# A transposed share moved ahead of its tick, and an early second load in the first image

## The chip, the cores and the metric

The kernel runs on one core of a Trainium2 chip. The metric is the time of one execution on the device in microseconds (us). Engines are named as the profile names them: PE (TensorE), PEld (its weight loads), DVE (VectorE), ACT (ScalarE), POOL (GpSimd) and SP, which here only issues DMAs. All data are 32-bit floats.

## The reference, cut to what matters

```python
# x: (4, 32, 128, 128).  Layer 0, for each of the 4 images:
xs = space_to_depth(x, 2)                  # (128 channels, 4096 positions), called q
energy = q.T-products / (|q_i| |q_j|)      # 4096 x 4096, cosine similarity of positions
attn = softmax(energy)                     # exp of it, divided by the row sums
x = gamma * (attn applied to q) + xs
# Layer 1: the tokens of the result
t = t + linear_attention(layer_norm(t))
t = t + top2_of_8_experts(layer_norm(t))
```

The energy matrix is symmetric, and so is its exponential. The kernel computes only one triangle of it and uses each off-diagonal tile twice: once as it is, and once transposed.

## The kernel before, in words

**Tiling.** The 4096 positions of an image are cut into 8 chunks of 512. `attend(b, st)` walks over rows i = 0 to 7 and in each over output tiles jc = 0 to i; a tile is worked off in four *ticks* j = 0 to 3, one for each block of 128 positions. A tick issues, in this order:

- on PE, `pe` (L609): the energy block, 128x512, from the normalised positions `qn`;
- on ACT, `pr` (L612): its exponential, with the row sum;
- what `turn_tick()` has due: `values` of the block two ticks earlier (L497, on PE, adds into the row's output bank `po`), and the DVE transposes of the block one tick earlier into a tile `F` (L421, L565), which a pair of DMAs through DRAM finishes transposing (L530 and L545, L554 for diagonal tiles);
- the clock's advance, and then `step_share()`, which may issue one step of a *transposed share*: a matmul of a finished `F` (L433, or L453 for a diagonal tile) with an ACT pass over it for the row sums (L438, L457).

Each fp32 product appears in the trace as two MATMUL records (x2).

**The row's bank.** There is one bank `po` (pool `ps_o`, one buffer). The last `values` of row i-1 is issued in tick 1 of row i, with the ACT copy of `po` to `o` (L502) behind it. The first `values` of row i is issued in tick 2 of the row's first output tile and needs the bank empty.

**The clock.** `clock[0]` counts work in units, not time. A tick adds `2 * (CH - c0) // P`, which is 8 for a full block and 8, 6, 4, 2 in the diagonal tile; a step of a share adds 4. A share is queued in `late` with a due value:

```python
late.append((at or clock[0] + LAG, transposed_share(b, st, i, jc, G)))   # LAG = 57
...
def step_share():
    if late and late[0][0] <= clock[0]:
        clock[0] += NJ
```

All other work (`prep` of further chunks, layer 1 of the image before) is a set of generators that the main loop steps by this clock. The list `timed` holds (generator, begin, end, count), with begin and end in per cent of an image's 1568 units; a due generator is stepped twice in a tick, ahead of the tick's work and after it. Layer 1's streams step once in 10 units.

**The start.** `prep_first` (chunks 0 and 1 of image 0, "the first pair") loads `xa` in quarters, turns it (L316), squares and sums it (L295, L296), takes the power -1/2 on POOL (L164), scales (L338), and transposes on PE (L344) with an ACT copy to `qn` (L342). `prep(0, 1, ...)` (chunks 2 and 3, "the second pair") does the same, but spreads its scale factors over PE (`wide` L388, `pnorm` L399) and scales on DVE in its own layout (L372). Both pairs' `xa` come from the pool `xin`, which has one buffer. `keep_running(40)` lets PE transpose the identity meanwhile (L186).

**Order.** Inside `tc.manual_schedule` PE, DVE, ACT and SP issue in the order of the program; outside it the scheduler chooses. Before, the first pair's work stands outside and the second pair's mostly inside.

Of the kernel before, what the change touches and what calls it, by code (L numbers as in the profile page):

```python
# [12 lines left out]
F32 = mybir.dt.float32  # L13
# [3 lines left out]
ALU = mybir.AluOpType  # L17
AX = mybir.AxisListType
# [4 lines left out]
def kernel(  # L23
# [43 lines left out]
    nc = tc.nc  # L67
    P = 128
# [5 lines left out]
    NJ = CH // P  # L74
    HW2 = W // 2
# [106 lines left out]
    def keep_running(n, pool=None, tag=None):  # L182

        bank = psum_t("spare") if pool is None else pool.tile([P, CH], F32, tag=tag, name="spare")
        for _ in range(n):
            nc.tensor.transpose(bank[:, :P], ident, ident)  # L186
# [95 lines left out]
    def chunks_of(b, kc, st):  # L282
        qT = qpool.tile([P, 2, NJ, P], F32, tag="qT", name=f"qT_{b}_{kc}")
        st.setdefault("qT", {})[2 * kc] = qT[:, 0]
        st["qT"][2 * kc + 1] = qT[:, 1]
        return qT
# [6 lines left out]
    def squares(b, kc, s, qT, ss):  # L293
        sq = work.tile([P, NJ, P], F32, tag="qs", name=f"sq_{b}_{kc}_{s}", bufs=2)
        nc.vector.tensor_tensor(sq, qT[:, s], qT[:, s], ALU.mult)  # L295
        nc.vector.tensor_reduce(ss[:, ts(s, NJ)], sq, AX.X, ALU.add)  # L296
# [2 lines left out]
        rows = st["T"][:, ts(kc, 8), :]  # L299
        return rows.rearrange("p k (w r) -> p k w r", r=2)  # L300

    def load_quarters(b, kc, queues=(nc.sync, nc.sync)):

        xa = xin.tile([P, 2, 2, 2, HW2, 2], F32, tag="xx", name=f"xa_{b}_{kc}")
        halves = x[b].rearrange("c (s g) w -> c s (g w)", s=2)
        for a in (0, 2, 1, 3):
            first_row = 16 * kc + 4 * a
            queues[a // 2].dma_start(
                xa[ts(a, S)].rearrange("p s k r w e -> p s (k r w e)"),
                halves[:, :, first_row * W : (first_row + 4) * W],  # L310
            )
        return xa

    def turn_quarters(s, xa, qT):
        for k in range(2):
            nc.vector.transpose(  # L316
                qT[:, s, 2 * k : 2 * k + 2, :].rearrange("p h (e r c) -> p r (h e) c", e=2, r=2),
                xa[:, s, k].rearrange("p r (h t) e -> p (r h) e t", h=2),
            )

    def prep_first(st):

        b, kc = 0, 0
        st["T"] = big1.tile([P, KT, D], F32, tag="T", name="T_0")
        xa = load_quarters(b, kc, (nc.sync, nc.scalar))
        qT = chunks_of(b, kc, st)
        yield
        ss = stat.tile([P, 2 * NJ], F32, tag="ss", name=f"ss_{b}_{kc}")
        rn = stat.tile([P, 2 * NJ, 1], F32, tag="rn", name=f"rn_{b}_{kc}")
        for s in range(2):  # L330
            turn_quarters(s, xa, qT)
            squares(b, kc, s, qT, ss)
            pow_neg_half(rn[:, ts(s, NJ), 0], ss[:, ts(s, NJ)])
        keep_running(40, ps_g, "pg")
        scaled = []
        for s in range(2):
            qs = work.tile([P, NJ, P], F32, tag="qs", name=f"qs_{b}_{kc}_{s}", bufs=2)
            nc.vector.tensor_tensor(qs, qT[:, s], rn[:, ts(s, NJ)].to_broadcast([P, NJ, P]), ALU.mult)  # L338
            scaled.append(qs)
        for s, qs in enumerate(scaled):  # L340
            qn = channels(b, kc, s, st)
            pt, done = hold(f"ptn_{b}_{kc}_{s}", lambda p, qn=qn: nc.scalar.activation(qn, p, AF.Copy))  # L342
            for j in range(NJ):
                nc.tensor.transpose(pt[:, ts(j, P)], qs[:, j, :], ident)  # L344
            done()
            yield

    def prep(b, kc, st):

        ahead = 2 if b == 0 and kc == 1 else 5
        xa = load_quarters(b, kc)
        if b == 0:
            load_tokens(st["T"][:, ts(kc, 8), :], b, 8 * kc, 8)
            xx = rows_of_image(b, kc, st)
        for _ in range(ahead):
            yield
        qT = chunks_of(b, kc, st)
        for s in range(2):  # L360
            turn_quarters(s, xa, qT)
            yield
        if b > 0:
            xx = xin.tile([P, 8, HW2, 2], F32, tag="xx", name=f"xx_{b}_{kc}")
            load_tokens(xx.rearrange("p k w r -> p k (w r)"), b, 8 * kc, 8)
        ss = stat.tile([P, 2 * NJ], F32, tag="ss", name=f"ss_{b}_{kc}")

        def scale(s, spread, view):
            qn = channels(b, kc, s, st)
            own = slice(s * 64, s * 64 + 64)  # L370
            for r2 in range(2):
                nc.vector.tensor_tensor(  # L372
                    qn[ts(r2, 64)].rearrange("p (j a t) -> p a j t", a=4, t=S),
                    xx[own].rearrange("p (a k) (h t) r -> p r a (k h) t", a=4, h=2)[:, r2],
                    view(spread[own]),
                    ALU.mult,
                )
        rn = stat.tile([P, 2 * NJ, 1], F32, tag="rn", name=f"rn_{b}_{kc}")
        for s in range(2):
            squares(b, kc, s, qT, ss)  # L380
            if s == 1:
                pow_neg_half(rn[:, :, 0], ss)
            yield
        for _ in range(ahead - 2):
            yield
        wide = work.tile([P, NJ, 2, 64], F32, tag="qs", name=f"wide_{b}_{kc}", bufs=2)
        for s in range(2):
            nc.vector.tensor_copy(wide[:, :, s], rn[:, ts(s, NJ)].to_broadcast([P, NJ, 64]))  # L388
        yield
        if b:  # L390
            yield

        def scale_all(bank):
            for s in range(2):
                scale(s, bank, lambda ap: ap.rearrange("p (j a t) -> p a j t", a=4, t=S))

        bank, done = hold(f"pnorm_{b}_{kc}", scale_all)
        for j in range(NJ):
            nc.tensor.transpose(bank[:, ts(j, P)], wide[:, j].rearrange("p s c -> p (s c)"), ident)  # L399
        yield  # L400
        done()
        yield
# [10 lines left out]
    def after(ticks, f):  # L413
        queued.append((tick[0] + ticks, f))

    def turn_tick():

        due = [f for at, f in queued if at <= tick[0]]
        queued[:] = [q for q in queued if q[0] > tick[0]]
        for f in due:  # L420
            f()  # L421
# [52 lines left out]
    def attend(b, st):  # L474
# [11 lines left out]
        for i in range(NCH):  # L486
# [94 lines left out]
            for jc in order:  # L581
# [21 lines left out]
                for j in range(NJ):  # L603
                    t = NJ * jc + j
                    c0 = 0 if jc < i else P * j
                    yield
                    tick[0] += 1
                    pe = ps_e.tile([P, CH], F32, tag="pe", name=f"pe_{b}_{i}_{t}")
                    nc.tensor.matmul(pe[:, c0:], qn[jc][:, ts(j, P)], qn[i][:, c0:], start=True, stop=True)  # L609
                    pr = ppool.tile([P, CH], F32, tag="pr", name=f"pr_{b}_{i}_{t}")  # L610
                    exps[:] = [
                        nc.scalar.activation(pr[:, c0:], pe[:, c0:], AF.Exp, accum_out=sums[:, t, i : i + 1]).ins  # L612
                    ]
                    own.append(pr)
                    if ending and jc == order[-1] and j == NJ - 1:
                        st["exps"] = True
                    after(2, partial(values, pr[:, c0:], t, c0, CH))
                    if jc < i and not both:
                        after(1, partial(nc.vector.transpose, Fb[:, :, :, j, :], pr))
                        if j == NJ - 1:  # L620
                            after(2, partial(move, F, i, jc))
                    elif jc == i and not ending:
                        if j < NJ - 1:
                            after(1, partial(turn_blocks, F, pr, j))
                        if j == NJ - 2:
                            after(2, partial(move_diagonal, F, i))
                    elif jc == i and j in (1, 2):

                        after(1 if j == 2 and order[-1] == i else 2, partial(below, own, (2, 1) if j == 1 else (3,)))
                    turn_tick()  # L630
                    clock[0] += 2 * (CH - c0) // P
                    step_share()
                    yield

    def finish():
# [767 lines left out]
    UNITS = 3 * NJ * NJ * NCH * (NCH - 1) // 2 + 7 * NJ * NCH  # L1403

    first, second = prep_first(states[0]), prep(0, 1, states[0])
    next(first)
    load_weights()
    next(first)
    next(second)
    load_tokens(states[0]["T"][:, 0:8, :], 0, 0, 8)  # L1410

    ordered = ExitStack()
    ordered.enter_context(tc.manual_schedule(engines=ENGINES))
    timed = [(first, 0, 1, 2), (second, 0.5, 5.5, 10)]
    for b in range(B):

        if b == 0:
# [80 lines left out]
```

## Time and profile before

| | |
|---|---|
| median of 3 runs | 1663.79 us (1658.05 to 1667.66) |
| the profiled execution: time / span | 1659.2 us / 1657.4 us |
| PE busy | 1623.1 us, 98% of the span |
| DVE, ACT busy | 55% and 55% |
| POOL busy | 36% |
| DMA | mean 201 GB/s |
| chain that ended last | 84% PE |

PE's busy time counts pipelined matmuls from start to modelled end, so it is not PE at its peak. What shows whether PE loses time is the distance between starts: in the dense stretches a 128x512 product takes 0.86 us (two passes of 0.43). A gap is read against that. The square brackets at the end of a timeline line give the idle time ahead of a group and what ended it.

### The profile page before, as it was taken

Reading aid. Unit: us, or ns where it says so; the run is one execution under the profiler, and the core shown is the slowest. Engines: PE = TensorE matmul, PEld = TensorE weight load, DVE = VectorE, ACT = ScalarE, POOL = GpSimd, SP = SyncE. Lnnn points to the kernel's source line nnn. Section 1 sums busy time; section 2 is a strip of 40 time slices with the busy share of each in tenths; the row PEclk is TensorE's granted clock in tenths of the full one; section 3 lists DMA queues with packets and bytes.
Section 4 is the critical chain, followed back from the end, with each engine's and each line's share of the span. In section 5 each row is a group of like instructions: output and inputs, shape, how many; then the busy total and the mean of one; then the engine's idle time right before and its main releaser. Section 6 shows DMA issues by size and latency. Waiting matters only on the chain.

```text
span 1657.4 us, 21471 instructions
## 1 busy us (share of the span) xinstructions
PE 1623.1 (98%) x5288; PEld 856.9 (52%) x5288; DVE 917.4 (55%) x2359; ACT 910.4 (55%) x2863; POOL 596.2 (36%) x565
## 2 busy tenths in 40 slices
PE   8999999999999999999999999999999999999987
PEld 5444544455554455555564455555565445554643
DVE  4543353567486443559378453448559533344686
ACT  3555445566575555556575455556657455555376
POOL 1000000001014531456555543346546642436166
PEclk9999999999999999999999999999999999999999
DMA  4555656665349776986778868797668877885001
GB/s 147 199 181 174 198 186 213 230 212 170 131 171 277 246 220 213 271 249 176 207 200 254 265 208 255 214 287 200 167 196 239 277 222 246 240 254 168 15 14 39
DMA packets 241899, 332.81 MB, mean 201 GB/s; under 512 B 31984, under 2 KB 168304, under 8 KB 227440
## 3 DMA queue, kind: packets, MB, share of 16 engines
q1 hardware_dynamic: 207312, 291.92, 55.5%
q0 software_dynamic: 26624, 25.58, 7.5%
q10 hardware_dynamic: 7840, 13.93, 2.8%
q8 instruction: 45, 0.74, 0.2%
q14 instruction: 78, 0.64, 0.1%
HBM read 160.78 MB, written 175.80 MB: 203 GB/s over the span
## 4 chain that ended last, share of the span: by engine, by line
PE 84%; DMA 4%; DVE 4%; SPq 3%; ACT 2%; issue 2%; another core or an unknown queue 1%; POOL 0%; ACTq 0%; DVEq 0%; POOLq 0%
PE po L497 24%; PE pe L609 23%; PE pg L433 20%; PE pys L1117 3%; DMA blocks<-F 3%; PE py L1290 3%; PE pg L453 2%; SPq L545 2%; PE pat L854 2%; PE pys L1124 2%; PE pgram L728 1%; PE ptx L701 1%; DVE df L761 1%; PE pgv L839 0%
## 5 line engine op out<-in xcount | busy, mean ns | idle before, releaser
L612 ACT ACTIVATE pr<-pe 128x512 f32<-128x512 f32 (+1 forms) x576 | 322.4, 560 | 544.0 <-PE pe L609 448.2
L497 PE MATMUL po<-pr,qT 128*128 128x512 f32 (+3 forms) x1152 | 549.6, 559 | 4.2 <-ACT o L502 3.0
L609 PE MATMUL pe<-qn,qn 128*128 128x512 f32 x896 | 459.6, 595 | 2.6 <-ACT pr L612 1.6
L433 PE MATMUL pg<-F,qT 128*128 128x512 f32 x880 | 449.7, 592 | 1.1 <-DMA F<-blocks 1.1
L421 DVE STREAM_TRANSPOSE F<-pr 128x512 f32<-128x512 f32 x440 | 305.9, 702 | 144.8 <-ACT pr L612 127.0
L497 PEld LDWEIGHTS po<-pr,qT 128*128 128x128 f32 x1152 | 215.3, 190 | 251.7 <-issue 221.2
L1165 POOL DMA_INDIRECT acc<-ys,place x128 | 203.2, 1588 | 215.8 <-ACT pr L612 140.3
L438 ACT ACTIVATE junk<-F 128x512 bf16<-128x512 f32 x440 | 273.0, 620 | 1.2 <-DMA F<-blocks 1.2
L433 PEld LDWEIGHTS pg<-F,qT 128*128 128x128 f32 x880 | 166.7, 190 | 195.4 <-issue 181.0
L1053 POOL DMA_INDIRECT xs<-xn,place x192 | 186.0, 969 | 189.7 <-ACT pr L612 116.6
L609 PEld LDWEIGHTS pe<-qn,qn 128*128 128x128 f32 x896 | 155.0, 191 | 115.0 <-issue 104.6
L442 DVE TENSOR_TENSOR o<-o,pg 128x512 f32<-128x512 f32 x110 | 75.3, 684 | 207.9 <-PE pg L433 173.4
L1099 DVE TENSOR_TENSOR results<-pys,xn 128x256 f32<-128x256 f32 x120 | 49.9, 416 | 187.1 <-ACT xn L1093 122.0
L164 POOL TENSOR_TENSOR rn<-ss,neg_half 128x8 f32<-128x8 f32 (+1 forms) x17 | 27.2, 1602 | 320.9 <-DVE ss L296 320.8
L612 ACT ACTIVATION_READ_ACCUMULATOR pr<-pe 128x1 f32 x576 | 112.0, 194 | 0.0
L1093 ACT ACTIVATE xn<-pys 128x256 f32<-128x256 f32 x120 | 45.2, 377 | 112.5 <-PE pys L1124 94.5
L1117 PEld LDWEIGHTS pys<-ew_sb,xn 128*128 128x128 f32 x468 | 70.4, 191 | 53.0 <-issue 49.5
L1165 POOL DMA_INDIRECT yb<-ys,place x64 | 61.8, 965 | 84.5 <-DMA F<-blocks 31.1
L609 PE MATMUL pe<-qn 128*128 128x512 f32 (+3 forms) x256 | 90.2, 435 | 0.7 <-ACT qn L342 0.7
L438 ACT ACTIVATION_READ_ACCUMULATOR junk<-F 128x1 f32 x440 | 84.6, 192 | 0.0
L1117 PE MATMUL pys<-ew_sb,xn 128*128 x468 | 71.7, 275 | 0.4 <-ACT xn L1093 0.4
L164 POOL TENSOR_TENSOR rsa<-dm_a,neg_half 128x8 f32<-128x8 f32 x16 | 28.9, 1807 | 103.1 <-DVE sv_a L688 102.9
(216 smaller groups left out, 1521.1 us busy)
## 6 DMA issues: line engine op xcount, KB each, us to landing
blocks<-F SPq DMA_DIRECT2D x110, 1024.0 KB
F<-blocks SPq DMA_DIRECT2D x220, 192.0 KB
F<-blocks SPq DMA_DIRECT2D x220, 128.0 KB
xn<-xs SPq DMA_DIRECT2D x114, 132.0 KB
ys<-results SPq DMA_DIRECT2D x114, 128.0 KB
F<-blocks SPq DMA_DIRECT2D x220, 64.0 KB
below<-F SPq DMA_DIRECT2D x31, 384.0 KB
T<-in_x_dram SPq DMA_DIRECT2D x64, 128.0 KB
```

Source lines behind the costliest of these rows:

```text
L164: pinned(nc.gpsimd.tensor_tensor(dst, src, neg_half.to_broadcast(list(src.shape)), ALU.pow))
L421: f()
L433: nc.tensor.matmul(pg.rearrange("p (a f) -> p a f", a=4), st["qT"][i][:, ib, :], G[:, :, ib], start=(ib == 0), stop=(ib == NJ - 1),)
L438: nc.scalar.activation(junk, G[:, :, ib], AF.Copy, accum_out=st["sums"][:, NJ * i + ib, jc : jc + 1])
L442: nc.vector.tensor_tensor(st["o"][jc], st["o"][jc], pg, ALU.add)
L497: nc.tensor.matmul(row["po"][:, lo:hi], qT[blk // NJ][:, blk % NJ, :], w, start=start, stop=(row["left"] == 0))
L609: nc.tensor.matmul(pe[:, c0:], qn[jc][:, ts(j, P)], qn[i][:, c0:], start=True, stop=True)
L612: nc.scalar.activation(pr[:, c0:], pe[:, c0:], AF.Exp, accum_out=sums[:, t, i : i + 1]).ins
L1053: inst = nc.gpsimd.indirect_dma_start(xs[h], offset(place[:, i, k : k + 1]), xn[:, k, :], None)
L1099: nc.vector.tensor_tensor(result[:, :n], p[:, 2 * P : 2 * P + n * D].rearrange("p (j c) -> p j c", c=D), bufs[g % 6][:, :n, D : D + 1].to_ ...
L1117: nc.tensor.matmul(p[:, 2 * P + j * D : 2 * P + j * D + D], bufs[6 + g % 2][:, j, :D], weights[:, bass.ds(begins[2 * (g % 2) + j], D)], st ...
L1165: inst = nc.gpsimd.indirect_dma_start(to, None, ys, offset(place[:, i, k : k + 1]), compute_op=op)
```

## The change

There are two parts.

1. In `attend`, in tick 2 of a row's first output tile (`jc == order[0] and j == 2`), `step_share()` is called ahead of `turn_tick()` and of the clock's advance. In all other ticks it stays behind them.
2. At the start of image 0 the second pair's quarters are loaded into a buffer of `work` with the tag "wide" instead of the single one of `xin`, and the load is issued ahead of the weights. Its four turns on DVE stand among the first pair's steps, its squares and sums directly behind them, and the part inside the hand-written order begins earlier. The first pair's scaled rows get buffers of the tag "grp". The second pair's remaining steps (`wide`, `pnorm`, scaling) start at 1.3% of the image instead of 0.5%, with 8 steps planned instead of 10.

```diff
--- before.py
+++ after.py
@@ -299,9 +299,9 @@
         rows = st["T"][:, ts(kc, 8), :]
         return rows.rearrange("p k (w r) -> p k w r", r=2)
 
-    def load_quarters(b, kc, queues=(nc.sync, nc.sync)):
-
-        xa = xin.tile([P, 2, 2, 2, HW2, 2], F32, tag="xx", name=f"xa_{b}_{kc}")
+    def load_quarters(b, kc, queues=(nc.sync, nc.sync), place=(xin, "xx")):
+
+        xa = place[0].tile([P, 2, 2, 2, HW2, 2], F32, tag=place[1], name=f"xa_{b}_{kc}")
         halves = x[b].rearrange("c (s g) w -> c s (g w)", s=2)
         for a in (0, 2, 1, 3):
             first_row = 16 * kc + 4 * a
@@ -311,12 +311,15 @@
             )
         return xa
 
+    def turn_quarter(s, k, xa, qT):
+        nc.vector.transpose(
+            qT[:, s, 2 * k : 2 * k + 2, :].rearrange("p h (e r c) -> p r (h e) c", e=2, r=2),
+            xa[:, s, k].rearrange("p r (h t) e -> p (r h) e t", h=2),
+        )
+
     def turn_quarters(s, xa, qT):
         for k in range(2):
-            nc.vector.transpose(
-                qT[:, s, 2 * k : 2 * k + 2, :].rearrange("p h (e r c) -> p r (h e) c", e=2, r=2),
-                xa[:, s, k].rearrange("p r (h t) e -> p (r h) e t", h=2),
-            )
+            turn_quarter(s, k, xa, qT)
 
     def prep_first(st):
 
@@ -327,16 +330,32 @@
         yield
         ss = stat.tile([P, 2 * NJ], F32, tag="ss", name=f"ss_{b}_{kc}")
         rn = stat.tile([P, 2 * NJ, 1], F32, tag="rn", name=f"rn_{b}_{kc}")
-        for s in range(2):
+        def rows_squared(s):
             turn_quarters(s, xa, qT)
-            squares(b, kc, s, qT, ss)
+            sq = work.tile([P, NJ, P], F32, tag="qs", name=f"sq_{b}_{kc}_{s}", bufs=2)
+            nc.vector.tensor_tensor(sq, qT[:, s], qT[:, s], ALU.mult)
+            return sq
+
+        def summed(s, sq):
+            nc.vector.tensor_reduce(ss[:, ts(s, NJ)], sq, AX.X, ALU.add)
             pow_neg_half(rn[:, ts(s, NJ), 0], ss[:, ts(s, NJ)])
-        keep_running(40, ps_g, "pg")
-        scaled = []
-        for s in range(2):
-            qs = work.tile([P, NJ, P], F32, tag="qs", name=f"qs_{b}_{kc}_{s}", bufs=2)
+
+        def scale_rows(s):
+            qs = work.tile([P, NJ, P], F32, tag="grp", name=f"qs_{b}_{kc}_{s}", bufs=2)
             nc.vector.tensor_tensor(qs, qT[:, s], rn[:, ts(s, NJ)].to_broadcast([P, NJ, P]), ALU.mult)
             scaled.append(qs)
+
+        scaled = []
+        keep_running(40, ps_g, "pg")
+        summed(0, rows_squared(0))
+        sq = rows_squared(1)
+        st["turns"].pop(0)()
+        scale_rows(0)
+        summed(1, sq)
+        st["turns"].pop(0)()
+        st["turns"].pop(0)()
+        scale_rows(1)
+        st["turns"].pop(0)()
         for s, qs in enumerate(scaled):
             qn = channels(b, kc, s, st)
             pt, done = hold(f"ptn_{b}_{kc}_{s}", lambda p, qn=qn: nc.scalar.activation(qn, p, AF.Copy))
@@ -349,15 +368,23 @@
 
 
 
-        ahead = 2 if b == 0 and kc == 1 else 5
-        xa = load_quarters(b, kc)
+        soon = b == 0 and kc == 1
+        ahead = 2 if soon else 5
+        if soon:
+            xa = load_quarters(b, kc, place=(work, "wide"))
+            yield
+        else:
+            xa = load_quarters(b, kc)
         if b == 0:
             load_tokens(st["T"][:, ts(kc, 8), :], b, 8 * kc, 8)
             xx = rows_of_image(b, kc, st)
-        for _ in range(ahead):
-            yield
         qT = chunks_of(b, kc, st)
-        for s in range(2):
+        if soon:
+            st["turns"] = [partial(turn_quarter, s, k, xa, qT) for s in range(2) for k in range(2)]
+            yield
+        for _ in range(0 if soon else ahead):
+            yield
+        for s in range(0 if soon else 2):
             turn_quarters(s, xa, qT)
             yield
         if b > 0:
@@ -387,8 +414,7 @@
         for s in range(2):
             nc.vector.tensor_copy(wide[:, :, s], rn[:, ts(s, NJ)].to_broadcast([P, NJ, 64]))
         yield
-        if b:
-            yield
+        yield
 
         def scale_all(bank):
             for s in range(2):
@@ -627,9 +653,13 @@
                     elif jc == i and j in (1, 2):
 
                         after(1 if j == 2 and order[-1] == i else 2, partial(below, own, (2, 1) if j == 1 else (3,)))
+                    starts = jc == order[0] and j == 2
+                    if starts:
+                        step_share()
                     turn_tick()
                     clock[0] += 2 * (CH - c0) // P
-                    step_share()
+                    if not starts:
+                        step_share()
                     yield
 
     def finish():
@@ -1403,15 +1433,17 @@
     UNITS = 3 * NJ * NJ * NCH * (NCH - 1) // 2 + 7 * NJ * NCH
 
     first, second = prep_first(states[0]), prep(0, 1, states[0])
-    next(first)
-    load_weights()
+    ordered = ExitStack()
     next(first)
     next(second)
+    load_weights()
+    ordered.enter_context(tc.manual_schedule(engines=ENGINES))
+    next(second)
+    next(first)
     load_tokens(states[0]["T"][:, 0:8, :], 0, 0, 8)
-
-    ordered = ExitStack()
-    ordered.enter_context(tc.manual_schedule(engines=ENGINES))
-    timed = [(first, 0, 1, 2), (second, 0.5, 5.5, 10)]
+    next(second)
+    next(second)
+    timed = [(first, 0, 1, 2), (second, 1.3, 5.5, 8)]
     for b in range(B):
 
         if b == 0:
```

More of the change, by code (lines that the diff above doesn't have):

```diff
@@ L356, in prep @@
             xx = rows_of_image(b, kc, st)
-        for _ in range(ahead):
+        qT = chunks_of(b, kc, st)
+        if soon:
+            st["turns"] = [partial(turn_quarter, s, k, xa, qT) for s in range(2) for k in range(2)]
             yield
-        qT = chunks_of(b, kc, st)
-        for s in range(2):
+        for _ in range(0 if soon else ahead):
+            yield
+        for s in range(0 if soon else 2):
             turn_quarters(s, xa, qT)
```

## The prediction

> **What bounds the kernel now.** First the page: PE is busy 98% of the span and is 84% of the chain that ended last.
>
> ```profile
> PE 1623.1 (98%) x5288; PEld 856.9 (52%) x5288; DVE 917.4 (55%) x2359; ACT 910.4 (55%) x2863; POOL 596.2 (36%) x565
> PE 84%; DMA 4%; DVE 4%; SPq 3%; ACT 2%; issue 2%; another core or an unknown queue 1%; POOL 0%; ACTq 0%; DVEq 0%; POOLq 0%
> ```
>
> So only time that PE stands still or runs slowly can be won; both parts of the change aim at such places. The second view is the timeline of PE at the start (start, us, operation, and in brackets the idle time before it).
>
> ```profile
> 18.40 0.38 PE L497 MATMUL po<-pr,qT 128*128 128x128 f32 x2
> 21.26 0.99 PE L399 MATMUL pnorm<-ident,wide 128*128 128x128 f32 x4 [2.48 <-DVE wide L388]
> 22.04 1.92 PE L609 MATMUL pe<-qn,qn 128*128 128x512 f32 x2
> 23.75 1.57 PE L497 MATMUL po<-pr,qT 128*128 128x512 f32 x2
> 25.16 1.02 PE L609 MATMUL pe<-qn,qn 128*128 128x512 f32 x2
> ```
>
> PE stops at 18.6 and waits for `wide`, the second pair's scale factors. Afterwards it is slow: from 22.04 to 23.75 and on to 25.16 two products take 3.12 us where dense ones take 2 x 0.86. The windows view says why: the granted clock is 0.50.
>
> ```profile
> 21.50:24.80 3.30, 3.30 (x8) 1.75 (x7) 2.78 (x5) 0.69 (x2) 0.00 (x0) 0.50 0.06 17
> 24.90:28.00 3.10, 3.10 (x8) 1.35 (x8) 1.61 (x3) 0.75 (x3) 0.00 (x0) 1.00 0.00 0
> ```
>
> (The columns: length, busy time of PE, PEld, DVE, ACT, POOL, then PEclk, DMA share, GB/s.) Third, a row's first tile, timeline at 96 us:
>
> ```profile
> 96.12 1.02 PE L609 MATMUL pe<-qn,qn 128*128 128x512 f32 x2
> 96.69 0.59 ACT L502 ACTIVATE o<-po 128x512 f32<-128x512 f32 x1
> 97.33 1.12 PE L497 MATMUL po<-pr,qT 128*128 128x512 f32 x2 [0.18 <-ACT o L502]
> 98.29 1.02 PE L433 MATMUL pg<-F,qT 128*128 128x512 f32 x2
> ```
>
> The tick's `pe` starts at 96.12, so dense pace would put `po` at 96.98; it starts at 97.33, when ACT has emptied the bank. Then the share starts 0.96 later instead of 0.86. The row's start costs 0.35 + 0.10 = 0.45 us. The share that could stand in the gap comes right behind it. Of the 32 rows, 17 show this picture (gap, then L433): 14 with 0.45, and the 3 whose row 0 follows another image, as at 359.20, with 0.77, together 8.6 us.
>
> **What the Trainium skill says.** "TensorE: Matmul & The Clock Gate", Part 1, says that an idle window of about 3.4 us halves PE's clock. The trace agrees: the stop of 2.6 us is followed by 3.3 us at 0.50. "SBUF — State Buffer", section "two separate sides", says that a GpSimd instruction and a VectorE one with two SBUF inputs exclude each other on a shared port. The trace fits: L164 took 1.34 us while L295 ran beside it and 1.01 us for the same shape alone. "DMA: Bandwidth & Descriptors", section "Issuing engines are not separate DMA queues", says that all queues share the same 16 engines, so the second pair's early load competes with the first's; here `T`'s loads do that already.
>
> **Part 2, the start, step by step.**
>
> *The load.* Eight quarters of 128 KB (1.05 MB) now come first. The windows view shows 225 GB/s in 2 to 4 us and 194 in 4 to 6; at 210, and with the first pair there at 5.5 us as now, the second takes 2.5 us more: 8.0. SP's queue issues four L308 (2.5 us in the trace) from 2.1 to 4.6 and then 8 `T` loads (0.5 to 0.9 us each), to about 9; `T` is first read by L372 near 18. ACT's queue keeps 5 issues. Nothing queued there waits. POOL's queue holds only the powers until 19 us.
>
> *DVE and POOL.* Starts in the DVE timeline give 0.35 us for a turn and 0.57 to 0.65 for a square, sum or scaling. From 5.66: two turns, square, sum end at 7.6; the power runs 7.7 to 8.7 (1.01). The third and fourth turn end at 8.2; the square has two SBUF inputs and I let it wait for POOL: 8.7 to 9.3. The second pair's first turn to 9.65 (its data came at 8.0). Then `qs` starts at 9.65 instead of 9.79. Sum to 10.9, power 11.0 to 12.0, two turns beside it, second `qs` at 12.1 instead of 12.20. If the port is no hindrance, both are 0.65 earlier. I take 0.1 to 0.65; the value used is 0.25. DVE's order is fixed now, so a late load would hold back everything behind that turn.
>
> *The second pair.* Behind it: one turn 0.35, squares and sums 4 x 0.6 to about 15.4, power 1.64 (the 128x8 row) to 17.2, `wide` 0.5 to 17.8. By the clock, `wide` now goes ahead of tick 1 of row 1 and `pnorm` ahead of tick 2, which is where `pnorm` stands now. PE gets there at 18.6 - 0.25 = 18.35. The wait of 2.6 us is gone, with 0.5 to spare; the transposes of row 0 (L565), queued on DVE behind the sums, have their `pr` since 15.1 at the latest and delay `wide` by at most 0.2 beyond the power. The four L372 (2.8 us) need only be done before row 2, which begins near 28.
>
> *Sum.* The wait, 18.62 to 21.26: 2.65. The slow clock: 3.12 - 1.72 = 1.40 for the two products and 0.33 in `pnorm` (0.99 for four transposes that take 0.66 at 10.54): 1.7. The earlier `qs`: 0.25. **4.6 us**, between 2.75 (0.1 + 2.65, if the clock halves elsewhere instead) and 5.0. Everything after is PE bound, so it reaches the end.
>
> **Part 1, the moved step: mostly inert.** `step_share` tests `late[0][0] <= clock[0]`. Behind the tick the clock has had 8 more units; ahead of it, not. I followed the two counters through all rows. In image 0, row 3, tick 2 the clock stands at 204 and the share is due at 209: behind the tick 212 passes, ahead of it 204 fails. In rows 4 to 7 the dues are 1 to 5 units ahead of the clock, the same in every image; row 0 of images 1 to 3 misses by 3, with 4 to come. So in all 17 rows with a gap the share is *not* issued in tick 2 but in tick 3, and `po` still follows `pe` directly. The gaps stay: 17 x, gain 0. Where the share *is* due in time (rows 1 and 2 of images 1 to 3), another share or work lies in the way already, and the trace shows no gap at 368 or 388: gain 0 too.
>
> What moves is a run of shares by one tick, until a tick without a share swallows it (in row 5, tick 0 of the fourth tile). PE's work is the same. ACT has 0.79 us per tick (0.60 + 0.19) against PE's 1.72 in the emptied ticks; DVE has a transpose of 0.70: hidden. L438 and the DVE add L442 move along with their matmul. SP's L530 and L545 are tied to ticks, not to the share. `F` is held one tick longer; its six buffers come round 6 or more ticks after the share, so L421 waits for none. Layer 1's streams step about 4% more often by the clock, which moves their matmuls past some row starts: five rows are now covered by such work (59.7, 463, 852, 1240, 1355 or so), each may lose its cover for 0.45 and others win one: +/- 1.5 us.
>
> **Sum.** The profiled execution took 1659.2 us (span 1657.4 and 1.8 around it), 4.6 below the median of 1663.79; the runs lie 9.6 apart. A gain of 4.6 would make it 1654.6, and the median **1659.2**.
>
> **Rivals.**
>
> *The hoist works after all* (the due is met, by a reading of the clock that I have wrong): the share's 0.86 us covers the gap of 0.35 to 0.67, and 8.6 more go: 1663.8 - 4.6 - 8.6 = 1650.6. For it: the trace shows the share right behind the gap. Against: the numbers 204 and 209.
>
> *The start gains nothing*, as PE stops elsewhere for as long (a wait for `pe`'s input or a cold clock at another window): 1663.8, with part 1's +/- 1.5. For it: PE already idles at 9.4 and 11.2.
>
> *The second pair's load holds up DVE* (slower). DVE's first foreign turn stands ahead of `qs`. `qs` then starts 0.35 after the landing, so each us after 9.4 delays everything by one, and the 4.35 us won at `pnorm` are used up at 13.8: from there it is slower. At 15, PE idles from 9.2 to past 15, and half a clock for 3.4 us costs 1.7 again: 1663.8 + 1.2 + 1.7 = 1666.7; beyond 1672 only if it lands near 20. Against it: 1.05 MB at 210 GB/s.
>
> **How the numbers follow.** A difference of 0.5% (8.3 us) is about what a measurement of this kernel can tell from no change. Chances: main case 0.66, hoist works 0.14, start gains nothing 0.12, load late 0.08. Faster by over 0.5% needs 1655.5: nearly all of the second case and the lower edge of the first, 0.20. Slower by over 0.5%: half of the last, 0.04. The rest, 0.76. The main case's own range is 1656 to 1663; to hold 8 in 10 with the spread of the runs, 1650.5 to 1666.
>
> **What would show it.** Right: no PE wait before `pnorm`, no PEclk of 0.50 before 30 us, row 2's first `pe` 4 to 5 us earlier than 32.3; at every later row `po` still waiting for L502 with 0.45 lost, and then `pe`, not L433, behind it. Wrong: L433 between `pe` and `po` in rows 3 to 7; a DVE wait for `xa` past 9 us; a median under 1655 or over 1666.

## The result and the profile after

| | before | after |
|---|---|---|
| median of 6 runs (range), us | 1663.91 (1658.05 to 1667.66) | 1685.71 (1679.89 to 1687.03) |
| profiled execution: time / span, us | 1659.2 / 1657.4 | 1679.9 / 1678.1 |

The change is slower: 1.0131 times the time of before, 95% interval 1.0105 to 1.0157, some 22 us. The forecast was 4.6 us faster. The experiments below ran in four groups, each on one chip. There the kernel before takes 1651 us (medians of the groups 1650.8 to 1651.0) and the changed kernel, in one group, 1671.7, a ratio of 1.0136 (1.0120 to 1.0151). Each run is set against runs of before in its own group.

The page of the kernel after, its lines of busy time and of the chain of waits:

```profile
PE 1625.3 (97%) x5288; PEld 855.0 (51%) x5288; DVE 920.7 (55%) x2359; ACT 911.6 (54%) x2863; POOL 591.2 (35%) x565
PE 79%; DVE 7%; DMA 5%; ACT 4%; issue 2%; SPq 1%; POOL 1%; another core or an unknown queue 0%; ACTq 0%; DVEq 0%; POOLq 0%
```

The work is the same (5288 matmuls, and within 0.4% as much busy time on PE, DVE and ACT), but PE's part of the chain has gone from 84% to 79% and DVE's from 4% to 7%. So PE waits more. The loss isn't at the start. The timeline of PE there, kernel after:

```profile
18.27 0.38 PE L523 MATMUL po<-pr,qT 128*128 128x128 f32 x2
18.49 0.60 PE L425 MATMUL pnorm<-ident,wide 128*128 128x128 f32 x4
18.92 1.02 PE L635 MATMUL pe<-qn,qn 128*128 128x512 f32 x2
19.79 1.03 PE L523 MATMUL po<-pr,qT 128*128 128x512 f32 x2
```

`pnorm` (L425, before L399) starts at 18.49 without a wait, and the next two products have starts 0.87 apart. The windows view (columns as before) has the clock at 1.00 there and behind it:

```profile
17.80:21.10 3.30, 3.30 (x14) 1.73 (x13) 2.71 (x5) 1.93 (x6) 0.00 (x0) 1.00 0.44 155
21.10:24.40 3.30, 3.30 (x9) 1.51 (x8) 2.99 (x7) 1.37 (x4) 0.00 (x0) 1.00 0.24 53
```

Row 2's first `pe` starts at 27.75 for 32.26. Nor is it at the start of the later rows; row 4 of image 0 after:

```profile
91.62 1.02 PE L635 MATMUL pe<-qn,qn 128*128 128x512 f32 x2
92.83 1.12 PE L523 MATMUL po<-pr,qT 128*128 128x512 f32 x2 [0.18 <-ACT o L528]
93.79 1.02 PE L635 MATMUL pe<-qn,qn 128*128 128x512 f32 x2
```

The gap stays (1.21 from `pe` to `po`), and `pe` follows, not the share: it came one tick later, as forecast. A table of the time between the `o` copies of neighbouring rows finds the loss: the start is 4.4 us shorter, most rows are equal, and eight rows of images 1 to 3 are 1.4 to 5.0 us longer: (1,2), (1,7), (2,2), (2,3), (2,7), (3,2), (3,3), (3,5), together 25. Three rows of the waits view, kernel after (us in all, times, longest), name what ends the stops:

```profile
DVE qT L315 <- DMA xa<-in_x_dram: 19.1, 3, 6.7
PE pbd L804 <- DVE rdx L782: 7.3, 5, 2.9
PE pys L1154 <- DMA xn<-xs: 5.9, 5, 1.7
```

`pbd` and `pys` belong to layer 1 of the image before, `xa` to the preparation of the next image. None of them is a step of either part of the change. One of the three waits for `xa`, 5.8 us, is the very start's, and the kernel before has that one alone; it has no such line for `pbd` and `pys`:

```profile
DVE qT L316 <- DMA xa<-in_x_dram: 5.7, 1, 5.7
```

**Back along the chain.** The stop of 2.80 us ahead of `pbd` at 782.47 (image 2, row 2), followed back in the chain of waits of the kernel after (start, us, what):

```profile
752.18 0.87 PE pe L635 x2
...
753.24 2.55 DMA acc<-t
...
755.86 0.34 SPq L580
...
756.24 0.58 SPq L308
...
758.14 2.76 DMA xa<-in_x_dram
...
761.09 1.42 DVE qT L315 x4
...
781.70 0.73 DVE rdx L782 x2
...
782.47 0.66 PE pbd L804 x4
```

Read from the top: ACT issues layer 1's fetch `acc<-t` (L1183) in its turn, behind a `pr` that waits for that `pe`. SP (SPq is its DMA queue) waits till it has landed, and only then issues `below<-F` (L580) and the quarters of `xa` (L308). DVE, whose order is fixed, stands 6.7 us at the turn L315 and from there is on the path for 21 us until it makes `rdx`. SP's own queue in the kernel after, and then in `start_only`, which has part 2 alone:

```profile
743.62 2.31 SPq L571 DMA_DIRECT2D F<-blocks  x5
755.86 0.34 SPq L580 DMA_DIRECT2D below<-F  x1
756.24 1.85 SPq L308 DMA_DIRECT2D xa<-in_x_dram  x3
```

```profile
746.61 0.37 SPq L580 DMA_DIRECT2D below<-F  x1
747.02 2.49 SPq L308 DMA_DIRECT2D xa<-in_x_dram  x4
```

After, SP's queue stands idle from 745.94 to 755.80; with part 2 alone `xa` is issued at 747.02. The waits view of SP's queue has this stop and one more like it:

```profile
SPq L580 <- DMA acc<-t: 21.4, 2, 11.5
```

The `xn<-xs` that `pys` waits for is a DMA of SP as well (L1113). It waits 10.8 us for `acc<-t` in the kernel after and not at all in `start_only`. SP's `below<-F` uses nothing of `acc<-t`. What ties them is in the operands of the trace: the DMAs of SP and of ACT take eight completion semaphores, 100 to 107, in turn in the order of the program, and each waits until the last DMA on its semaphore is done:

```
753.24  ACT  acc<-t                    signals 106
755.80  SP   wait for 106
755.86  SP   below<-F                  signals 106
756.24  SP   xa<-in_x_dram             signals 107
756.86  SP   xa<-in_x_dram             signals 100
```

So a DMA that ACT issues late, since ACT follows PE, holds a queue that otherwise runs ahead. "DMA: Bandwidth & Descriptors" in the Trainium skill, section "Why a DMA increments its semaphore by 16 and not by 1", says why there is a wait: two DMAs in flight on one semaphore would fill each other's count. The trace shows the wait, not this reason for it. That the holder can be another engine's DMA is seen here: 2.55 us of flight, and before it the wait for ACT's turn.

### The profile page after: what moved, and what is told of

The parts are those of the page before. It is cut to its first block, busy times and chain, and to the rows that moved or that the text cites. A ratio compares the mean times of both kernels' runs of the same rounds, so it can differ in the third digit from the quotient of the medians.

```text
span 1678.1 us, 21473 instructions
## 1 busy us (share of the span) xinstructions
PE 1625.3 (97%) x5288; PEld 855.0 (51%) x5288; DVE 920.7 (55%) x2359; ACT 911.6 (54%) x2863; POOL 591.2 (35%) x565
## 4 chain that ended last, share of the span: by engine, by line
PE 79%; DVE 7%; DMA 5%; ACT 4%; issue 2%; SPq 1%; POOL 1%; another core or an unknown queue 0%; ACTq 0%; DVEq 0%; POOLq 0%
PE po L523 23%; PE pe L635 22%; PE pg L459 19%; PE pys L1147 3%; PE py L1320 3%; PE pg L479 2%; PE pys L1154 2%; PE pgram L758 1%; ACT xn L726 1%; DMA F<-blocks 1%; PE pat L884 1%; ACT pr L638 1%; DMA xn<-xs 1%; DVE df L791 1%; POOL rsf L164 1%
```

## The experiments

The theory after the result: the skipped share leaves the clock 4 units lower for stretches, and that clock paces everything else, not the shares alone. The rivals: the moved shares themselves, the two parts together, or another place. All edits are to the changed kernel, or to `start_only` where it says so. The us are differences of medians, against before in the same group.

| run | us over before | ratio (95%) |
|---|---|---|
| start_only | -3.5 | 0.9978 (0.9971 to 0.9985) |
| share_only | +26.2 | 1.0156 (1.0141 to 1.0172) |
| start_after_pace | +6.8 | 1.0051 (1.0036 to 1.0067) |
| due_share | -11.2 | 0.9934 (0.9920 to 0.9948) |
| row_0_only | +8.8 | 1.0056 (1.0039 to 1.0073) |
| rows_from_2 | +16.5 | 1.0101 (1.0084 to 1.0118) |
| prep_early | +18.3 | 1.0112 (1.0094 to 1.0130) |
| start_pace8 | +11.4 | 1.0068 (1.0051 to 1.0085) |
| after_again | +20.8 | 1.0136 (1.0120 to 1.0151) |
| after_fetch_pool | +4.5 | 1.0032 (1.0019 to 1.0045) |
| start_fetch_pool | -0.9 | 0.9993 (0.9985 to 1.0002) |
| due_fetch_pool | -10.1 | 0.9938 (0.9924 to 0.9951) |
| fetch_pool_prep_early | +4.9 | 1.0027 (1.0017 to 1.0036) |

**The parts alone.** `start_only` is the changed kernel with the one `step_share()` behind the tick as before; `share_only` is the kernel before with this edit alone:

```diff
+                    starts = jc == order[0] and j == 2
+                    if starts:
+                        step_share()
                     turn_tick()
                     clock[0] += 2 * (CH - c0) // P
-                    step_share()
+                    if not starts:
+                        step_share()
```

> The changed kernel with step_share() back behind the clock's advance in every tick; the early load and the new start stay. If the moved share step is what costs (pace or displacement): the median is 1663.9 - 4.5 = 1659.4, no later row loses anything against before. If the start itself disturbs what comes later (buffers, order on SP): about 1685, as the changed kernel.

> The kernel before with only the moved share step. If the two parts add up: 1685.7 + 4.5 = 1690. If the moved step is harmless and the loss comes from the start or from the two together: about 1664.

Part 2 gains 3.5 us, part 1 loses 26.2. So the loss is part 1's, and it comes with the old start too (`pbd` waits 7.9 us there, `pys` 6.5).

**The clock without the shares.** In `start_after_pace` (from `start_only`) the shares are issued as before; a second counter runs as the changed kernel's clock would, and the preparation and layer 1 are stepped by it.

```diff
+    pace = [0]
+    paced = []
+
+    def step_pace():
+        if paced and paced[0][0] <= pace[0]:
+            pace[0] += NJ
...
-                t = 100 * (clock[0] - start) / UNITS
+                t = 100 * (pace[0] - start) / UNITS
...
-                    if clock[0] >= stream[1]:
-                        stream[1] = clock[0] + PACE
+                    if pace[0] >= stream[1]:
+                        stream[1] = pace[0] + PACE
```

> As start_only, with the shares issued where the kernel before issues them; but the main loop steps prep and layer 1 by a second clock that counts as the changed kernel's does (in tick 2 of a row's first tile it tests before it advances). Theory pace (layer 1's steps fall into other ticks and its waits land on PE): about 1684, near the changed kernel, though no share is displaced. Theory displacement (shares one tick later no longer fill PE's waits, or make layer 1 wait for its rows): 1659 as start_only.

It is 10.3 us slower than `start_only` with every share in its old place. So the pace alone costs, but not the whole 24.3 us between `start_only` and `after_again`: `pys` waits 4.6 us in it, `pbd` not at all, and DVE's wait for `xa` is 7.1 us for 19.1. The hold on SP's queue is there too, at another place: `xn<-xs` waits 4.2 us for `acc<-t`. The other half, shares a tick late and pace as before, wasn't tried, so whether the remaining 14.0 us come from the late shares by themselves or only from both together stays open.

**The share really ahead.** In `due_share` the early test is made against the clock as it will stand behind the tick, so a share that is due in this tick goes ahead of `po`:

```diff
-    def step_share():
-        if late and late[0][0] <= clock[0]:
+    def step_share(ahead=0):
+        if late and late[0][0] <= clock[0] + ahead:
...
-                        step_share()
+                        step_share(2 * (CH - c0) // P)
```

> The changed kernel, but the step ahead of turn_tick() is tested against what the clock will be at the end of its tick, so the share is due and is issued between pe and po. The clock at the end of each tick, and with it all steps of prep and layer 1, is as before. Both theories: the 17 gaps of 0.45 to 0.77 us are filled, 1659.4 - 8.6 = 1650.8. If the gap only moves behind the share (the bank is emptied later, or pe waits): 1659.

The timeline of PE in `due_share`, at the same row start as above:

```profile
91.75 1.02 PE L635 MATMUL pe<-qn,qn 128*128 128x512 f32 x2
92.61 1.02 PE L459 MATMUL pg<-F,qT 128*128 128x512 f32 x2
93.47 1.02 PE L523 MATMUL po<-pr,qT 128*128 128x512 f32 x2
```

Starts 0.86 apart: the gap is gone. Against `start_only` it gains 7.75 us, and the distances between PE's starts, less the dense pace and added up from 30 us to the last `o` copy, fall by some 8 us. So a share ahead of `po` does no harm where the clock keeps its old course; the share that fails its test, and leaves the clock lower, comes with the loss.

**Where the early test hurts.** `row_0_only` and `rows_from_2` make the early test in some rows only:

```diff
-                    starts = jc == order[0] and j == 2
+                    starts = jc == order[0] and j == 2 and i == 0      # row_0_only
+                    starts = jc == order[0] and j == 2 and i >= 2      # rows_from_2
```

> The changed kernel with the early test in row 0 only. Row 0 of images 1 to 3 is where the skipped share leaves the clock 4 units lower for some ten ticks, so the next chunk's pnorm and four scalings (L399) come a tick later, in row 2's tick 0, right ahead of close_rows' sums on DVE. If this collision makes the PE waits for rdx (9 us in share_only, and some 4 more of half clock or late po): about 13 to 16 us over start_only, that is 10 to 13 over before. If the loss is spread over all rows with a skipped share: a fifth of 29, 2 to 3 over before at most.

> The changed kernel with the early test only in rows 2 to 7; the boundary between images keeps its order. Collision theory: no PE wait for rdx; what stays is layer 1 stepped 2 to 3% more often (waits of pys for the gathered xn, 5 to 7 us, and of pe for ACT, 2): about +4 to +6 over before. If the loss is spread over all rows: +18 or more over before.

`row_0_only` loses somewhat less than was expected, and `rows_from_2` is a miss by far. Both contain the gain of the start; against `start_only` they lose 12.3 and 20.0 us, 32.3 together, where the changed kernel, which has row 1 besides, loses 24.3. So no single row is the culprit, and the losses don't add. That how the streams lie to each other after the shift decides is a guess that fits; it isn't shown. In `row_0_only` DVE's wait for `xa` is 6.2 us, hardly more than the start's, so its loss has another path, which wasn't followed. The waits view of `rows_from_2` shows the late `xa` again, without row 0:

```profile
DVE qT L315 <- DMA xa<-in_x_dram: 17.0, 3, 5.9
```

**Two attempts at the streams.** `prep_early` begins the second stream of the preparation at 0.25% of the image for 0.5%; `start_pace8` (from `start_only`) steps layer 1 once in 8 units:

```diff
-            timed.append((prep(b + 1, 2, nxt), 0.5, 16, 17))
+            timed.append((prep(b + 1, 2, nxt), 0.25, 16, 17))
```
```diff
-    PACE = 10
+    PACE = 8
```

> The changed kernel with one number changed: the third pair of the next image begins at 0.25% instead of 0.5% of an image, 4 clock units sooner, which is what the skipped share takes away; its scalings are then back in row 1's last tick. All shares and layer 1's pace stay as in the changed kernel (about +22 over before). Collision theory: the waits for rdx and the half clock behind them go, 9 to 13 us less: about +10 over before. If displaced shares themselves make PE wait: still +20 or more.

> start_only with layer 1 stepped every 8 clock units instead of 10, so also in ticks without a share (in the emission order image 1's stream is at its 128th step where it was at its 115th, and at its 120th in the changed kernel). No share is moved. Theory that pace alone costs: pys waits for the gathered xn (0.6 us in start_only, 6 to 8 in the others), +5 to +12 over before. If pace is harmless and only the coincidence with moved shares costs: -3.5 as start_only.

`prep_early` is the second miss: `pbd` still waits 7.3 us for `rdx`, `qT` 19.5 for `xa`. Beginning a load earlier doesn't help where its queue is held; SP's queue in `prep_early` stands from 745.14 to 757.53:

```profile
743.73 1.41 SPq L571 DMA_DIRECT2D F<-blocks  x3
757.53 0.34 SPq L580 DMA_DIRECT2D below<-F  x1
```

`start_pace8` is slower by as much as was foreseen, but not at `pys`, where it was foreseen, and elsewhere than in the changed kernel (waits view):

```profile
PE pgram L754 <- ACT xn L722: 8.6, 2, 4.5
PE pnorm L425 <- DVE wide L415: 4.0, 3, 2.0
```

More steps of layer 1 cost time, but they don't make the stops of the changed kernel.

**The fetch off ACT's queue.** `after_again` is the changed kernel unaltered. `after_fetch_pool`, `start_fetch_pool` and `due_fetch_pool` issue layer 1's fetch from POOL, whose DMAs take eight other semaphores (111 to 118 in the trace):

```diff
-                nc.scalar.dma_start(accs[g], t2[:, ts(g, 4)])
+                pinned(nc.gpsimd.dma_start(accs[g], t2[:, ts(g, 4)]))
```

> The changed kernel once more, unaltered, so that its trace and time stand beside the next three on one chip. Expected: +21 to +23 over before, and in the trace SP waiting for the DMA acc<-t ahead of L580 and of L1189, then DVE waiting for xa.

> The changed kernel with one line changed: layer 1's fetch (acc<-t) is issued from POOL's queue instead of ACT's, in order with the gathers that use it. Theory semaphores: the DMAs of SP and ACT take eight completion semaphores in turn, in the order of the program, and each waits until the last DMA on its semaphore is done; layer 1 stepped earlier puts an acc<-t that waits for a free buffer ahead of SP's below<-F and xa, and SP stands for 12 us. Then with acc<-t out of that turn the waits of DVE for xa (2 x 6.7 us) and of PE for rdx (7 us) go: about 10 to 16 us less than after_again. Rival (displaced shares or layer 1's pace reach PE directly): within 4 us of after_again.

> Control: start_only with the same line changed. In start_only acc<-t also holds SP (some 80 us in all) but DVE and PE don't wait for it. Theory semaphores: little changes, -3.5 over before, within 2 of start_only. If the fetch on POOL is worth something by itself, it shows here too.

> due_share (share issued between pe and po, -11.2 against before) with the fetch on POOL. Both theories: -11 to -13; slower than due_share if POOL's queue, waiting for the fetch's buffer, delays the gathers that layer 1 ends with.

The one line takes 16.3 us off the changed kernel and adds 2.6 to the one with part 2 alone (within 2 was expected), so 18.9 of the 24.3 us hang on it. The waits view of `after_fetch_pool`:

```profile
DVE qT L315 <- DMA xa<-in_x_dram: 5.9, 1, 5.9
PE pbd L804 <- DVE rdx L782: 3.2, 3, 1.2
```

The wait for `xa` is down to the one at the very start, `pys` no longer waits, and `pbd` waits 3.2 us for 7.5. SP's queue, which waits 113.6 us in all for `acc<-t` in `after_again`, has no such wait left. The line also takes the fetch out of ACT's order, but that is not seen to help: ACT's two longest waits for another engine than PE stay as they were (33.4 us in all in `after_again` and 32.5 here, 14.8 and 14.8). This shows the hold to be the main cause. With the share placed rightly the same line gains nothing (`due_fetch_pool` against `due_share`: about 1 us slower, which is within the intervals). In `start_only` SP waits 89.0 us for `acc<-t` without harm to `xa`, so what counts is which DMA stands behind the hold, not its length.

**The rest.** 5.3 us are left between `after_fetch_pool` and `start_fetch_pool`. In `after_fetch_pool`, `den`, from which `rdx` is made, stands on DVE right behind four scalings (L399, 2.77 us). The last run begins these earlier, by `prep_early`'s edit on top of `after_fetch_pool`.

> The changed kernel with layer 1's fetch on the POOL queue (measured at 4.5 us over before) and, besides, the second stream of a pair's preparation begun a quarter of a tick earlier (0.25 for 0.5). Theory: what is left of the loss is a matter of where the preparation's steps fall: den stands right behind the four scalings of the next queries on VectorE, because these come one tick late at a clock that is 4 lower, and TensorE's pbd waits 3.2 us in all for rdx. With the steps begun earlier that wait is gone or under 1 us and the time falls by 2 to 4 us, to +0.5 to +2.5 over before. Rival: the rest is the load of the streams themselves (more of layer 1 and of the preparation in the same ticks), which an earlier begin doesn't remove: the wait moves to another product and the time stays at +4 to +6.

It brings nothing (+4.9 for +4.5), and `pbd` waits 3.0 us for 3.2. The timeline of DVE in it, and then in `after_fetch_pool`:

```profile
770.65 2.74 DVE L399 TENSOR_TENSOR qn<-xx,pnorm 64x512 f32<-64x512 f32 x4
773.41 0.87 DVE L816 BATCH_NORM_STATS2 bs_a<-T 128x6 f32<-128x128 f32 x4
...
775.76 0.22 DVE L777 TENSOR_REDUCE den<-sums 128x8 f32<-128x72 f32 x1
```

```profile
770.79 0.66 DVE L816 BATCH_NORM_STATS2 bs_a<-T 128x6 f32<-128x128 f32 x3
...
772.80 2.77 DVE L399 TENSOR_TENSOR qn<-xx,pnorm 64x512 f32<-64x512 f32 x4
775.60 0.23 DVE L777 TENSOR_REDUCE den<-sums 128x8 f32<-128x72 f32 x1
```

The scalings did move, 2.15 us ahead, and other queued work took their place; `den` came no earlier. So `den` standing right behind the scalings is not the cause of the rest. That the amount of DVE work in these ticks is the cause fits both timelines; it was not tested, and the rest stays open.

## Why the prediction was wrong

**Part 2 was right.** Forecast 4.6 us, in the trace 4.5 (27.75 for 32.26), in time 3.5 (2.5 to 4.8 by the interval of `start_only`). In the kernel after there is no wait at `pnorm`, no half clock and no late load on DVE: the forecast's slower rival, the second pair's load, didn't occur. The half clock does come back in other traces of the same start. In four of thirteen (`start_only`, `start_after_pace`, `start_pace8`, `due_fetch_pool`) the granted clock is 0.50 to 0.65 from 12.9 to 15.8 us, behind a stop of 2.1 to 2.6 us ahead of `ptn` (the first pair's transposes; 1.2 to 1.8 us in the others), and row 2's first `pe` starts at 29.15 to 29.43; in the other nine it is 1.00 there, and `pe` starts at 27.70 to 28.03. So the gain at the start is some 3 us in some executions and 4.2 to 4.6 in others, which fits the 3.5 in time. That is the forecast's own lower edge, the clock that "halves elsewhere instead". One step on the way came right by luck. The first `qs` starts at 9.70 for 9.65, but the sum ahead of it ends at 8.02 for 7.6, and the square that was to wait for POOL doesn't: it starts at 8.73, beside the power on POOL (8.17 to 9.21), and takes its usual 0.69. The two errors nearly cancel.

**The hoist was inert, as worked out.** Shares missed the early test and went a tick later. Of the 17 gaps 15 stayed, 0.35 us each and 0.67 in the three of row 0. Two (row 7 of images 1 and 2) were covered by `pys` products of layer 1, and two of 0.28 opened (row 4 of images 2 and 3), the exchange that the forecast allowed for. The rival that it works was also sized well: 8.6 us forecast, 7.75 measured in `due_share`, once the test looks ahead by the tick's 8 units.

**The step that failed** is the term "Layer 1's streams step about 4% more often ... +/- 1.5 us". The count was right: followed through the counters, image 1's layer 1 stands at its 120th step in row 7 of the next image where it stood at its 115th. The price was wrong. I priced only the cover that these matmuls give to gaps at row starts. I didn't ask what else the steps issue and what is queued behind that: their DMA on ACT's queue, and SP's queue behind it. With these steps and no share moved the loss is 10.3 us (`start_after_pace` less `start_only`). With the shares a tick late as well, which the forecast put at nothing ("hidden"), it is 24.3 (`after_again` less `start_only`); 18.9 of these hang on the fetch's place among the DMAs, 5.3 don't. The sum should have read 1663.8 - 4 + 24, and not - 4.6 +/- 1.5.

**A second sentence failed with it**: "SP's L530 and L545 are tied to ticks, not to the share". They are, in the order of the program; but their time depends on whatever DMA used their semaphore last. The forecast gave SP's queue behind the start no price at all. In the kernel before its waits do no harm to `xa`, which DVE waits for only at the very start. The slower cases of the forecast were a late load at the start and the +/- 1.5 us; none was a stream that shifts and holds another's DMAs.

**A reading of the clock.** The forecast took the stop of 2.6 us and the 0.50 behind it to agree with an idle window of about 3.4 us. The stop is shorter than that, so the traces don't show the length. Nor does the length of a stop settle it: in the kernel after, the stop of 2.80 us ahead of 782.47 has a granted clock of 1.00 in the window around it (779.00 to 782.40) and in the next (782.40 to 785.80).

**What could have been seen.** Nothing in the profile of before shows the stops of the kernel after, as they didn't occur. What it does show is the tie itself, in the waits view of SP's queue:

```profile
SPq L530 <- DMA acc<-t: 39.2, 9, 9.6
```

L530 writes an `F` to DRAM and reads nothing of `acc<-t`. A long wait between two transfers that share no data is the sign of a shared resource, and should have widened the range upwards.

## What to carry to other kernels

A counter that decides when one thing is issued often paces others: before a test on it is moved, list everything that reads it and price each reader's DMAs, not its matmuls alone. Moving a test ahead of an update needs the test to look ahead by that update; here this is the difference between 21 us lost and 11 us won, and `due_share` (0.9934 of before, interval 0.9920 to 0.9948) is the version to keep. Where a queue waits for a transfer that it has no use for, look at which semaphore the two share.

## What was not expected of the hardware and the program on it

SP's and ACT's DMAs are not independent here, since they take eight completion semaphores in turn: one `acc<-t` of 2.55 us held SP's queue idle for 9.9 us (745.94 to 755.80), and the transfer of `xa` behind it was late enough to put DVE, busy 55% of the span, on the path for 21 us. The same fetch on POOL's queue changed the time by -16.3 us in one kernel, by +2.6 and about +1 in two others (the last within the noise), so it is no rule to issue it there.
